# Sums of log decays: loaded broadcast for each unit, or multiplied out on TensorE (gated linear attention with a mixture of experts)

## The chip, the cores and the metric

The kernel runs on one core of a Trainium2 chip. The metric is the device time of one launch in microseconds (us); a smaller time is better. Engines are named as the profile names them: PE (TensorE), DVE (VectorE), ACT (ScalarE), POOL (GpSimd) and SP (SyncE, which here only issues DMAs). Each engine works through its own instructions in a fixed order, and stands still while the next one in that order waits.

## The reference

The input `x` has 4 sequences of 2048 tokens of 256 numbers. A layer norm gives `xn`, and the output is `x + attention(xn) + experts(xn)`. The attention is gated and linear: 8 heads, keys of 128, values of 64, and one decay per token and head.

```python
q = (x @ Wq).reshape(B, S, H, DK)
k = (x @ Wk).reshape(B, S, H, DK) * DK ** (-0.5)
v = (x @ Wv).reshape(B, S, H, DV)
alpha = jax.nn.sigmoid((x @ Wg + bg) / GATE_NORM)

def step(state, inp):
    qt, kt, vt, at = inp
    state = at[..., None, None] * state + kt[..., None] * vt[:, :, None, :]
    out_t = jnp.einsum('bhk,bhkv->bhv', qt, state)
    return (state, out_t)
...
og = jax.nn.sigmoid(x @ Wog)
return out * og @ Wo
```

The experts are 64 small gated networks (256 to 128 to 256). A router picks 8 of them for each token, an expert takes at most the first 256 tokens that picked it, and the weighted results are added to the output.

## The kernel before

**Chunked attention.** The scan is done in chunks of 128 tokens. With `L(t)` the running sum of log decays inside a chunk, the product of query `i` and key `j` of one chunk is weighted by `exp(L(i) - L(j))` where `i >= j` and by zero elsewhere. What a chunk passes on is a state of 128 by 64 for each head.

**Blocks, units, half blocks.** `block(s)` (line 1031) runs 32 times, each time over 256 tokens, which are two chunks (`ck` 0 and 1), for two halves of four heads (`half` 0 and 1). The pair (half, chunk) of a block is a *unit*: there are 128 units. A block is software pipelined in two half blocks; each ends with `outputs(done)` for two units. For one unit the work is: `unit_l` (the decay matrix `dc`, 128 keys by 4 heads by 128 queries, fp32), `unit_a` (the scores `sp` on PE), `unit_m` (line 929, DVE: `dc = sp * dc`), and in `outputs` the products of `dc` with the values and of the state with `qt` (lines 945 and 951). Around them are `keys` and `queries` (projections `pj`, each split on ACT and DVE into two fp16 parts, lines 220 and 221), `turn_keys` (transposes `kp`), `states`, `split_o` (`oh` on ACT, `ol` on POOL or DVE) and `output`.

**The decay matrix before.** `decays(gi)` makes the sums for a group of batches (`DGROUPS`; one batch is 512 tokens): it splits the log decays on a grid, sums them with PE, cuts the sums into three bf16 parts, turns them and stores them in DRAM as `lt_d`; `exp` of the sums goes to `el_d`. `load_block` (line 783) loads the parts of queries and keys into rows of `mv` and `aj`, whose other rows hold -1, 1 and 0. `unit_l` then multiplies the two, 128 by 128 by 512 in bf16 (`lp`, line 899): that gives all differences `L(i) - L(j)`. ACT applies Relu with scale -1 and then Exp with scale -1 (lines 903 and 904), and a mask clears `i < j`: POOL's `affine_select` (line 909) in the first 16 blocks, a DVE multiply by `u_le` (line 907) from then on.

**Loads broadcast over partitions.** `load_el` (line 798) loads `el`, the factors that queries are multiplied by (`qt`, line 860): one row in DRAM is copied to all 128 partitions, 512 KB for half a block. There are three buffers, so that such a load waits until an earlier `qt` has been made. `wall` (line 866) is the last column of `el`.

**Stages.** While blocks 0 to 15 run, side jobs run between their steps: `front(b)` (layer norm, split, transposes, stores), `decays` and `back(b)` (the router). After them the bank pools of PSUM are shared anew (`share_banks(3)`: three banks for `pj` in place of four), and the 64 experts run between the steps of blocks 16 to 31. Before block 0 lies a prologue in which the weights are scaled and split.

**What sets the order.** The program states work in the order of the calls; a scheduler places each instruction on its engine's queue by its own simulated times, and `tc.issue_after` ties some to others. All loads and most stores are issued on SP, in one queue. Each DMA there uses one of eight completion semaphores in turn, and waits until the DMA eight places earlier has landed.

Of the kernel before, what the change touches and what calls it, by code (L numbers as in the profile page):

```python
# [8 lines left out]
F32 = mybir.dt.float32  # L9
F32R = mybir.dt.float32r  # L10
F16 = mybir.dt.float16
BF16 = mybir.dt.bfloat16
# [30 lines left out]
CGRID = 1.5 * 2.0 ** 14  # L43
# [5 lines left out]
NPART = 3  # L49
NJ = NPART * H  # L50
KL = 2 * NJ + 2 * NPART

# [19 lines left out]
def gla_moe_kernel(ctx: ExitStack, tc: tile.TileContext, x, Wq, Wk, Wv, Wo, Wg, bg, Wog,  # L72
# [17 lines left out]
    lt_d = [dram.tile([2 * NPART, H, RT, P], BF16, name=f"lt_d{b}") for b in range(NB)]  # L90
# [4 lines left out]
    identb = const.tile([P, P], BF16, name="identb")  # L95
    nc.vector.tensor_copy(identb, ident)
# [15 lines left out]
    w_end = const.tile([P, NB, H, RT], F32, name="w_end")  # L112
# [9 lines left out]


    mz = tmpc.tile([P, H], BF16, name="mz")
    nc.vector.memset(mz, 0.0)
    for q0 in (0, NJ + 2 * NPART):
        for m in range(NPART):
            nc.gpsimd.affine_select(out=mz, in_=mz, pattern=[[-1, H]],
                                    compare_op=ALU.not_equal, fill=-1.0, base=-(q0 + 8 * m),
                                    channel_multiplier=1)  # L130
    NM = 4

    mv_t = [const.tile([P, H, P], BF16, name=f"mv{i}") for i in range(NM)]
    aj_t = [const.tile([P, NCK, P], BF16, name=f"aj{i}") for i in range(2)]
    nc.gpsimd.tensor_copy(mv_t[0], bc(mz, 2, P))
    for t in aj_t:
        nc.vector.memset(t, 1.0)
# [111 lines left out]
    dcp = ctx.enter_context(tc.tile_pool(name="dcp", bufs=2))  # L249
# [33 lines left out]

    lad = r1.tile([P, RT, P], BF16, name="lad")
# [26 lines left out]
    zs = r1.tile([P, NB, H, RT], F32, name="zs")  # L311
    sg = r1.tile([P, NB, H, RT], F32, name="sg")
# [20 lines left out]
    def front(b):  # L333
# [79 lines left out]
        nc.vector.scalar_tensor_tensor(zs[:, b].rearrange("p h t -> p t h"), in0=lg[:, :, E:E + H],  # L413
# [8 lines left out]
    def decays(gi):  # L422

        b0, nb_ = DGROUPS[gi]
        n = nb_ * H * RT

        z = zs[:, b0:b0 + nb_].rearrange("p b h t -> p (b h t)")
        sm = sg[:, b0:b0 + nb_].rearrange("p b h t -> p (b h t)")
        nc.vector.tensor_scalar(sm, sm, SMIN, None, ALU.max)
        made["ln"] = nc.scalar.activation(sm, sm, AF.Ln).ins  # L430
        nc.vector.tensor_scalar(z, z, -UMIN, 0.0, ALU.add, ALU.min)
        nc.vector.tensor_scalar(z, z, LMIN - UMIN, None, ALU.max)
        yield True
        nc.vector.tensor_tensor(z, z, sm, ALU.add)

        g = dk.tile([P, 2, n], F32, tag="g", name="g")
        nc.vector.tensor_scalar(g[:, 0, :], z, CGRID, CGRID, ALU.add, ALU.subtract)
        made["g"] = nc.vector.tensor_tensor(g[:, 1, :], z, g[:, 0, :], ALU.subtract).ins
        yield True
        cs = ps["mo"].tile([P, 4, n], F32, tag="mo", name="cs")  # L440
        nc.tensor.matmul(cs[:, 0:2, :].rearrange("p a n -> p (a n)"), lhsT=u_le,
                         rhs=g.rearrange("p a n -> p (a n)"), start=True, stop=True)
        for q in range(2):
            nc.tensor.matmul(cs[:, 3, :], lhsT=u_le, rhs=g[:, q, :], start=(q == 0), stop=(q == 1))
        made["cs"] = nc.tensor.matmul(cs[:, 2, :], lhsT=u_gt, rhs=z, start=True, stop=True).ins

        le = dk.tile([P, n], F32, tag="le", name="le")
        made["le"] = nc.scalar.activation(le.rearrange("p (b t h) -> p b h t", b=nb_, t=RT),
                                          cs[:, 3, :].rearrange("p (b h t) -> p b h t", b=nb_, t=RT), AF.Exp).ins
        made["exp"] = nc.scalar.activation(w_end[:, b0:b0 + nb_].rearrange("p b h t -> p (b h t)"),  # L450
                                           cs[:, 2, :], AF.Exp).ins
        lt = dk.tile([P, 2, nb_, NPART, H * RT], BF16, tag="lt", name="lt")
        rs = dk.tile([P, 2, n], F32, tag="g", name="rs")
        by_batch = dict(b=nb_)
        c4 = cs[:, 0:2, :].rearrange("p a (b n) -> p a b n", **by_batch)
        r4 = rs.rearrange("p a (b n) -> p a b n", **by_batch)
        nc.vector.tensor_copy(lt[:, :, :, 0, :], c4)
        nc.vector.tensor_tensor(r4, c4, lt[:, :, :, 0, :], ALU.subtract)
        nc.vector.tensor_copy(lt[:, :, :, 1, :], r4)
        nc.vector.tensor_tensor(r4, r4, lt[:, :, :, 1, :], ALU.subtract)  # L460
        made["lt2"] = nc.vector.tensor_copy(lt[:, :, :, 2, :], r4).ins
        yield True
        ep = ps["mo"].tile([n, P], F32, tag="mo", name="ep")
        nc.tensor.transpose(ep, le, ident)
        els = dk.tile([n, P], F32, tag="ls", name="els")
        nc.vector.tensor_copy(els, ep)
        nc.sync.dma_start(out=el_d[gi], in_=els)
        NR = NPART * H * RT
        for i in range(nb_):
            b = b0 + i  # L470
            lp = ps["mo"].tile([NR, 2, P], BF16, tag="mo", name="ltp")
            for q in range(2):
                made["ltp"] = nc.tensor.transpose(lp[:, q, :], lt[:, q, i].rearrange("p a n -> p (a n)"), identb).ins
            lts = r2.tile([NR, 2, P], BF16, name="lts")
            made["lts"] = nc.vector.tensor_copy(lts, lp).ins
            made["lt"] = nc.sync.dma_start(out=lt_d[b].rearrange("(q a) h c i -> (a h c) q i", q=2), in_=lts).ins
            yield True
# [305 lines left out]
    def load_block(s):  # L783
        if s:
            begin_block(s)
        b, c0 = s // 2, (s % 2) * NCK
        aj = aj_t[s % 2]
        lt = lt_d[b].rearrange("a h c i -> (a h) c i")
        nc.sync.dma_start(out=aj[0:NJ], in_=lt[0:NJ, c0:c0 + NCK, :])
        nc.sync.dma_start(out=aj[NJ + 2 * NPART:KL], in_=lt[NJ:2 * NJ, c0:c0 + NCK, :])  # L790
        mv = []
        for ck in range(NCK):
            t = mv_t[(s * NCK + ck) % NM]
            loaded = nc.sync.dma_start(out=t[NJ:NJ + 2 * NPART], in_=lt_d[b][:, :, c0 + ck, :])
            mv.append(t)
        blk[s].update(loaded=loaded, aj=aj, mv=mv)
# [32 lines left out]
    def values(s, ck):  # L829

        B = blk[s]
        b, c0 = s // 2, (s % 2) * NCK
        xh, xl = B["x"]
        vp = ps["pj"].tile([P, H, DV], F32, tag="pj", name="pj")
        for c in range(2):
            product(vp.rearrange("p h v -> p (h v)"), (xh[:, ck, c, :], xl[:, ck, c, :]),
                    (wparts["wv"][0][:, c, :], wparts["wv"][1][:, c, :]), c == 0, c == 1)
        v = vp_.tile([P, H, DV], F32, name="v")
        nc.scalar.activation(v, vp, AF.Copy, scale=VFIT)
        B["v"][ck] = v  # L840
        if (s * NCK + ck + 1) % (SEQ // P):
            vwh = vp_.tile([P, H, DV], F16, name="vwh")
            vwl = vp_.tile([P, H, DV], F16, name="vwl")
            vw = w1.tile([P, H, DV], F32, name="vw")
            B["aux"].tensor_tensor(vw, v, bc(w_end[:, b, :, c0 + ck], 2, DV), ALU.mult)
            nc.scalar.copy(vwh, vw)
            B["aux"].tensor_tensor(vwl, vw, vwh, ALU.subtract)
            B["vw"][ck] = (vwh, vwl)

# [44 lines left out]
    def unit_l(s, half, ck):  # L894

        B = blk[s]
        h0 = half * 4
        lp = ps["pj"].tile([P, 4, P], F32, tag="pj", name="lp")
        nc.tensor.matmul(lp.rearrange("p h i -> p (h i)"), lhsT=B["aj"][:, ck, :],  # L899
                         rhs=B["mv"][ck][:, h0:h0 + 4, :].rearrange("p h i -> p (h i)"),  # L900
                         start=True, stop=True)
        dc = dcp.tile([P, 4, P], F32, name="dc")
        nc.scalar.activation(dc, lp, AF.Relu, scale=-1.0)
        nc.scalar.activation(dc, dc, AF.Exp, scale=-1.0)

        if "at" in moe:
            nc.vector.tensor_tensor(dc, dc, bc(u_le, 1, 4), ALU.mult)
        else:
            nc.gpsimd.affine_select(out=dc, in_=dc, pattern=[[0, 4], [1, P]], compare_op=ALU.is_ge,
                                    fill=0.0, base=0, channel_multiplier=-1)  # L910
# [120 lines left out]
    def block(s):  # L1031
# [8 lines left out]
        if n:  # L1040
            load_block(s + 1)
            load_el(s + 1, 0)
# [31 lines left out]
        if not n:  # L1074
# [7 lines left out]
            return  # L1082
        load_el(s + 1, 1)
# [35 lines left out]
    for t in mv_t[1:]:  # L1119
        nc.sync.dma_start(out=t, in_=mv_t[0])  # L1120
# [54 lines left out]
    with after(made["el"]):  # L1175
        load_block(0)
    with after(blk[0]["loaded"].ins):
        load_el(0, 1)
        nc.sync.dma_start(out=gbias, in_=gate_bias.partition_broadcast(P))
# [13 lines left out]
    with after(blk[0]["loaded"].ins):  # L1193
# [72 lines left out]
```

## Time and profile before

| | |
|---|---|
| median of 3 runs | 1252.58 us (1251.79 to 1253.54) |
| profiled execution: time | 1252.01 us |
| profiled execution: span on the core | 1250.0 us |
| granted clock of PE, mean | 0.995 |
| busy: PE, DVE, ACT, POOL | 1191.4, 973.5, 857.5, 709.3 us |
| moved by DMA | 165.35 MB |

The profile is of one execution. Its span of 1250.0 us is the part in which the core's engines run; 2.0 us lie around it. Busy time of PE counts each matmul from its start to its modelled end, and matmuls overlap, so that a duration is longer than the step from one start to the next. A line of a group reads: line of the kernel, engine, operation, output<-inputs, shape and type, count, then busy time, mean duration in ns, and the idle time of the engine just before these instructions with what ended it.

### The profile page before, as it was taken

Reading aid. Unit: us, or ns where it says so; the run is one execution under the profiler, and the core shown is the slowest. Engines: PE = TensorE matmul, PEld = TensorE weight load, DVE = VectorE, ACT = ScalarE, POOL = GpSimd, SP = SyncE. Lnnn points to the kernel's source line nnn. Section 1 sums busy time; section 2 is a strip of 40 time slices with the busy share of each in tenths; the row PEclk is TensorE's granted clock in tenths of the full one; section 3 lists DMA queues with packets and bytes.
Section 4 is the critical chain, followed back from the end, with each engine's and each line's share of the span. In section 5 each row is a group of like instructions: output and inputs, shape, how many; then the busy total and the mean of one; then the engine's idle time right before and its main releaser. Section 6 shows DMA issues by size and latency. Waiting matters only on the chain.

```text
span 1250.0 us, 34808 instructions
## 1 busy us (share of the span) xinstructions
PE 1191.4 (95%) x13783; PEld 1040.7 (83%) x13783; DVE 973.5 (78%) x2669; ACT 857.5 (69%) x1536; POOL 709.3 (57%) x899
## 2 busy tenths in 40 slices
PE   6799999989999999999899999999999999999997
PEld 6587888877888878878789989999988898998986
DVE  6987778786787877777878878787878788887674
ACT  4567666666667567654667777777777777778764
POOL 1476667765666566653426656637757567565330
PEclk9899999999999999999999999999999999999999
DMA  7434444434334443323637676767767678666531
GB/s 244 158 123 127 131 122 117 126 87 114 97 112 127 135 127 110 108 52 78 181 87 152 163 160 137 169 151 178 157 156 167 148 167 180 150 138 150 111 60 35
DMA packets 148579, 165.35 MB, mean 132 GB/s; under 512 B 32384, under 2 KB 119296, under 8 KB 147712
## 3 DMA queue, kind: packets, MB, share of 16 engines
q1 hardware_dynamic: 114896, 113.57, 29.6%
q0 software_dynamic: 29712, 45.89, 21.5%
q10 hardware_dynamic: 3808, 3.67, 0.8%
q8 instruction: 108, 1.77, 0.6%
q14 instruction: 55, 0.45, 0.1%
HBM read 115.98 MB, written 58.38 MB: 139 GB/s over the span
## 4 chain that ended last, share of the span: by engine, by line
PE 68%; DVE 13%; POOL 6%; ACT 5%; DMA 5%; issue 3%; SPq 1%; DVEq 0%; POOLq 0%; ACTq 0%
PE pj L269 11%; PE pj L271 11%; PE pj L270 11%; PE od L945 4%; PE kp L884 3%; PE od L951 3%; DMA el<-el_d 3%; PE gu L269 2%; PE gu L271 2%; PE gu L270 2%; PE xet L646 2%; PE sp L270 2%; PE sp L269 2%; PE sp L271 2%; PE lp L899 1%
## 5 line engine op out<-in xcount | busy, mean ns | idle before, releaser
L702 POOL DMA_INDIRECT out_dram<-y,idx x128 | 211.6, 1653 | 93.1 <-issue 25.4
L626 POOL DMA_INDIRECT xe<-xw_d,idx x128 | 133.5, 1043 | 127.2 <-ACT y L688 86.9
L269 PE MATMUL pj<-xs,wq_h 128*128 128x256 f16 x496 | 135.4, 273 | 6.6 <-DVE k L221 4.6
L269 PE MATMUL pj<-xs,wk_h 128*128 128x256 f16 x496 | 135.6, 273 | 0.0
L271 PE MATMUL pj<-xs,wk_l 128*128 128x256 f16 x496 | 135.5, 273 | 0.0
L270 PE MATMUL pj<-xs,wk_h 128*128 128x256 f16 x496 | 135.5, 273 | 0.0
L270 PE MATMUL pj<-xs,wq_h 128*128 128x256 f16 x496 | 135.2, 273 | 0.0
L271 PE MATMUL pj<-xs,wq_l 128*128 128x256 f16 x496 | 135.2, 273 | 0.0
L929 DVE TENSOR_TENSOR dc<-sp,dc 128x512 f32<-128x512 f32 x128 | 87.7, 685 | 45.8 <-PE sp L271 28.4
L221 DVE SCALAR_TENSOR_TENSOR k<-pj,k 128x512 f16<-128x512 f32 x128 | 87.1, 683 | 40.1 <-ACT k L220 40.1
L220 ACT ACTIVATE k<-pj 128x512 f16<-128x512 f32 x128 | 75.2, 591 | 55.4 <-PE pj L271 55.1
L945 PE MATMUL od<-dc,v 128*64 128x128 f32 x1024 | 101.5, 280 | 7.3 <-DVE dc L929 7.3
L270 PE MATMUL sp<-ql,k 128*128 128x128 f16 x512 | 96.1, 220 | 5.5 <-DVE ql L221 5.2
L269 PE MATMUL sp<-qh,k 128*128 128x128 f16 x512 | 98.2, 220 | 0.0
L271 PE MATMUL sp<-qh,k 128*128 128x128 f16 x512 | 96.1, 220 | 0.0
L220 ACT ACTIVATE qh<-pj 128x512 f16<-128x512 f32 x128 | 76.0, 597 | 27.0 <-PE pj L271 26.8
L951 PE MATMUL od<-qt,state 128*64 128x128 f32 x960 | 94.4, 273 | 0.0
L989 ACT CAST oh<-oT 128x512 fp32r<-128x512 f32 x64 | 39.6, 618 | 79.5 <-DVE oT L959 79.5
L221 DVE SCALAR_TENSOR_TENSOR ql<-pj,qh 128x512 f16<-128x512 f32 x128 | 86.8, 679 | 9.2 <-ACT qh L220 9.1
L716 DVE TENSOR_TENSOR wl<-w,wh 128x768 fp32r<-128x768 f32 x64 | 61.2, 956 | 40.9 <-ACT wh L650 39.3
L884 PE MATMUL kp<-identh,k 128*128 128x128 f16 x1024 | 83.0, 220 | 8.7 <-DVE k L221 5.4
L860 DVE SCALAR_TENSOR_TENSOR qt<-pj,el 128x512 f32<-128x512 f32 x128 | 86.7, 678 | 0.0
(408 smaller groups left out, 4533.6 us busy)
## 6 DMA issues: line engine op xcount, KB each, us to landing
el<-el_d SPq DMA_DIRECT2D x64, 512.0 KB
xw_d<-x SPq DMA_DIRECT2D x16, 512.0 KB
xT_d<-xT SPq DMA_DIRECT2D x16, 512.0 KB
out_dram<-in_L_attn_x_dram SPq DMA_DIRECT2D x16, 512.0 KB
w<-in_L_ffn_w_gate_dram SPq DMA_DIRECT2D x64, 128.0 KB
w<-in_L_ffn_w_up_dram SPq DMA_DIRECT2D x64, 128.0 KB
w<-in_L_ffn_w_down_dram SPq DMA_DIRECT2D x64, 128.0 KB
xs<-xT_d SPq DMA_DIRECT2D x31, 256.0 KB
```

The lines of the kernel that those rows point to most:

```text
L220: return (nc.scalar.activation(hi, t, AF.Copy, scale=scale).ins, nc.vector.scalar_tensor_tensor(lo, in0=t, scalar=scale, in1=hi, op0=ALU.m ...
L221: nc.vector.scalar_tensor_tensor(lo, in0=t, scalar=scale, in1=hi, op0=ALU.mult, op1=ALU.subtract).ins)
L269: nc.tensor.matmul(out_, lhsT=a[0], rhs=b[0], start=first, stop=False)
L270: nc.tensor.matmul(out_, lhsT=a[0], rhs=b[1], start=False, stop=False)
L271: return nc.tensor.matmul(out_, lhsT=a[1], rhs=b[0], start=False, stop=last).ins
L626: in_turn(lambda: nc.gpsimd.indirect_dma_start(out=xe[:, f, :], out_offset=None, in_=xw_d[:, :], in_offset=bass.IndirectOffsetOnAxis(ap=id ...
L702: two = [in_turn(lambda: nc.gpsimd.indirect_dma_start(out=of, out_offset=bass.IndirectOffsetOnAxis(ap=idx[:, e, f:f + 1], axis=0), in_=m[" ...
L860: read = nc.vector.scalar_tensor_tensor(qt, in0=pj, scalar=QFIT, in1=two_heads(el, i), op0=ALU.mult, op1=ALU.mult)
L884: nc.tensor.transpose(kp[:, i, :], k[:, i, :], identh)
L929: anchor.append(nc.vector.tensor_tensor(dc, B["sp"], dc, ALU.mult).ins)
L945: mm = nc.tensor.matmul(od[i * DV:(i + 1) * DV, n, j, :], lhsT=v[:, h0 + 2 * j + i, :], rhs=dc[:, 2 * j + i, :], start=True, stop=first)
L951: mm = nc.tensor.matmul(od[i * DV:(i + 1) * DV, n, j, :], lhsT=state[half][:, 2 * j + i, :], rhs=qt[:, ck, 2 * j + i, :], start=False, sto ...
```

## The change

`decays` no longer splits the sums. With the log decays `z` (tokens by batch, chunk and head) it makes three sums with PE in fp32: after the token (`w_end` as before), up to the token (`el` as before), and `nl`, which is minus the sum from the start of the token's own group of 32 keys (`GQ` = 4 groups of `Q` = 32). One more product, `z` against a constant `tq`, gives for each of the four groups the sum from the group's start to the query, and it is stored in DRAM as `la_d`. `load_la` copies the rows of one unit to the partitions: four DMAs of 64 KB, each of 2 KB to 32 partitions. `unit_l` masks the loaded tile first (to -3e4; POOL as before, or a DVE minimum), and then takes four Exps of 128 columns, one for each head, with `nl` as bias. The matmul `lp`, the Relu, the tiles `mv` and `aj` and their loads are gone. The tile `la` takes the place of `dc` and has six buffers in place of two. In `block`, `load_la` is called for the units two half blocks ahead.

```diff
-        g = dk.tile([P, 2, n], F32, tag="g", name="g")
-        nc.vector.tensor_scalar(g[:, 0, :], z, CGRID, CGRID, ALU.add, ALU.subtract)
-        made["g"] = nc.vector.tensor_tensor(g[:, 1, :], z, g[:, 0, :], ALU.subtract).ins
...
+        cs = ps["mo"].tile([P, 3, n], F32, tag="mo", name="cs")
+        for k, u in enumerate((u_gt, u_le, uq)):
+            made["cs"] = nc.tensor.matmul(cs[:, k, :], lhsT=u, rhs=z, start=True, stop=True).ins
...
+        made["lt2"] = nc.vector.tensor_copy(nl[:, b0:b0 + nb_].rearrange("p b t h -> p (b t h)"), cs[:, 2]).ins
...
+        lp = ps["mo"].tile([n, GQ, P], F32, tag="mo", name="lap")
+        made["ltp"] = nc.tensor.matmul(lp.rearrange("n g i -> n (g i)"), lhsT=z,
+                                       rhs=tq.rearrange("p g i -> p (g i)"), start=True, stop=True).ins
+        las = dk.tile([n, GQ, P], F32, tag="las", name="las")
+        made["lts"] = nc.vector.tensor_copy(las, lp).ins
+        made["lt"] = nc.sync.dma_start(out=la_d[gi].rearrange("g n i -> n g i"), in_=las).ins
...
-        for ck in range(NCK):
-            t = mv_t[(s * NCK + ck) % NM]
-            loaded = nc.sync.dma_start(out=t[NJ:NJ + 2 * NPART], in_=lt_d[b][:, :, c0 + ck, :])
...
+    def load_la(s, half, ck):
+
+        b, c = s // 2, (s % 2) * NCK + ck
+        la = lap.tile([P, 4, P], F32, name="la")
+        gi = max(i for i, g in enumerate(DGROUPS) if g[0] <= b)
+        r = ((b - DGROUPS[gi][0]) * RT + c) * H + half * 4
+        src = la_d[gi][:, r:r + 4, :].rearrange("g h i -> g (h i)")
+        for g in range(GQ):
+            made["la"] = nc.sync.dma_start(out=la[g * Q:(g + 1) * Q].rearrange("p h i -> p (h i)"),
+                                                 in_=src[g].partition_broadcast(Q)).ins
+        sums[s, half, ck] = la
...
     def unit_l(s, half, ck):
...
-        nc.tensor.matmul(lp.rearrange("p h i -> p (h i)"), lhsT=B["aj"][:, ck, :],
-                         rhs=B["mv"][ck][:, h0:h0 + 4, :].rearrange("p h i -> p (h i)"),
-                         start=True, stop=True)
-        dc = dcp.tile([P, 4, P], F32, name="dc")
-        nc.scalar.activation(dc, lp, AF.Relu, scale=-1.0)
-        nc.scalar.activation(dc, dc, AF.Exp, scale=-1.0)
-
+        b, c = s // 2, (s % 2) * NCK + ck
+        dc = sums.pop((s, half, ck))
         if "at" in moe:
-            nc.vector.tensor_tensor(dc, dc, bc(u_le, 1, 4), ALU.mult)
+            nc.vector.tensor_tensor(dc, dc, bc(later_, 1, 4), ALU.min)
         else:
             nc.gpsimd.affine_select(out=dc, in_=dc, pattern=[[0, 4], [1, P]], compare_op=ALU.is_ge,
-                                    fill=0.0, base=0, channel_multiplier=-1)
+                                    fill=NONE, base=0, channel_multiplier=-1)
+        for i in range(4):
+            hh = half * 4 + i
+            nc.scalar.activation(dc[:, i], dc[:, i], AF.Exp, bias=nl[:, b, c, hh:hh + 1])
...
         if n:
-            load_block(s + 1)
+            begin_block(s + 1)
...
+            load_la(s + 1, 0, 1)
+            load_la(s + 1, 1, 0)
             load_el(s + 1, 0)
...
+        load_la(s + 1, 1, 1)
+        if 0 < s < NS - 2:
+            load_la(s + 2, 0, 0)
         load_el(s + 1, 1)
...
-    for t in mv_t[1:]:
-        nc.sync.dma_start(out=t, in_=mv_t[0])
```

In the changed program's queues, each new tile's loads on SP wait for the `outputs` products that last read its buffer, those of the half block just ended. Its mask stands a few instructions behind the following `ol` (on DVE in the stage of the experts, on POOL before it), and its four Exps stand on ACT between the splits of keys and queries of that same half block, two half blocks before `unit_m` uses them.

## The prediction, made before the changed kernel ran

> **What bounds the kernel now.** I read the busy times first, then the stages, then the chain of waits.
>
> ```profile
> PE 1191.4 (95%) x13783; PEld 1040.7 (83%) x13783; DVE 973.5 (78%) x2669; ACT 857.5 (69%) x1536; POOL 709.3 (57%) x899
> core 0: us, PE busy (x) PEld busy (x) DVE busy (x) ACT busy (x) POOL busy (x), PEclk, DMA share, GB/s
> 50.10:604.60 554.50, 522.86 (x6284) 441.99 (x6285) 435.72 (x1278) 359.90 (x646) 344.65 (x602) 0.99 0.40 115
> 604.60:1208.80 604.20, 601.91 (x6835) 541.29 (x6833) 477.50 (x1219) 452.11 (x815) 351.96 (x262) 1.00 0.66 149
> PE 68%; DVE 13%; POOL 6%; ACT 5%; DMA 5%; issue 3%; SPq 1%; DVEq 0%; POOLq 0%; ACTq 0%
> ```
>
> PE carries the chain: 68% of the span, and in the stage of the experts (604.6 to 1208.8) it is never without a matmul. Before that stage (50.1 to 604.6) PE is covered to 94% only, and DVE, POOL, ACT and DMAs stand on the chain between its pieces. In both stages DVE and ACT have a fifth or more of their time free.
>
> Next the rows that the change touches, from the groups, and how matmuls follow each other, from the timeline of PE.
>
> ```profile
> L904 ACT ACTIVATE dc<-dc 128x512 f32<-128x512 f32 x128 | 81.2, 634 | 2.2
> L903 ACT ACTIVATE dc<-lp 128x512 f32<-128x512 f32 x128 | 76.1, 595 | 14.3 <-PE lp L899 14.3
> L899 PE MATMUL lp<-mv,aj 128*128 128x512 bf16 x128 | 49.3, 386 | 0.0
> L907 DVE TENSOR_TENSOR dc<-dc,u_le 128x512 f32<-128x512 f32 x63 | 43.2, 686 | 4.3 <-ACT dc L904 3.7
> 831.94 0.38 PE L899 MATMUL lp<-mv,aj 128*128 128x512 bf16 x1
> 832.15 0.27 PE L269 MATMUL pj<-xs,wk_h 128*128 128x256 f16 x1
> ```
>
> `lp` is listed with 386 ns, but the next matmul starts 0.21 us after it. So 49.3 us is not what its removal can give: 128 x 0.215 us = 27.5 us is.
>
> **The change, part by part.**
>
> *PE.* 128 `lp` go: 65 up to the expert stage (14.0 us of steps), 60 in it (12.9), 3 at the end. The pieces of the chain, summed by stage, hold 5.9 us of `lp` before the expert stage, 11.6 in it and 1.1 after it. I take the chain's numbers; the ends are 27.5 us (all of it) and 0 (something else is late at once). The sums in `decays` change by a few matmuls for six groups: nothing. `pj` has one tile less to pass through its banks for each unit. In the half block after 831 us the second product of queries starts at 839.67, 0.12 us after DVE released a `pj` bank (838.86 + 0.69): with three banks such a wait is near, and without `lp` the bank is one product older (some 1.4 us). That is slack for what follows, not time by itself.
>
> *ACT.* Relu and Exp of 512 columns follow each other by 0.48 and 0.53 us: 1.01 us a unit. Four Exps of 128 columns take their place, each with a bias read from SBUF. The nearest row has the shape, a read pointer (as scale) and SBUF as source:
>
> ```profile
> 13.01 0.39 ACT L220 ACTIVATE gwz<-gate_f,fit 128x128 f16<-128x128 f32 x1
> 13.30 0.29 ACT L220 ACTIVATE gwz<-wg_f,fit 128x16 f16<-128x16 f32 x1
> ```
>
> The next starts 0.29 us later: 4 x 0.29 = 1.16 us, 0.15 more a unit, 19 us in all. The ends are 4 x 0.10 (64 columns without a pointer, 129.22 to 129.32) and 4 x 0.49 (256 columns with two pointers, line 386), that is -78 and +122 us of ACT. ACT has 1250.0 - 857.5 = 392 us free, so 0 on the path; without that cover 19 us.
>
> *Masks.* The DVE minimum costs what the multiply did (686 ns), POOL's select what it did (636 ns): 0. But they now stand ahead of the Exps, and wait for a DMA.
>
> *DVE in `decays`.* Five cuts and two grid steps a group and sixteen copies of about 0.28 us go, six larger copies come: some 11 us less, off the path, 0.
>
> *DMA.* 128 tiles of 256 KB are 33.5 MB, less 1.6 MB of parts: 32 MB more. The queue moved 113.57 MB in 29.6% of the engines' span, so 8.3% more; the share in the expert stage goes from 0.66 to about 0.75. No engine is full: 0 by itself.
>
> *SP.* 512 issues of about 0.42 us (as `w` loads follow each other) replace 128 of 0.35 to 0.76: 215 against 71 us, and SP does nothing else. Moved past on its queue are `el`, `xs` and the experts' `w` loads. The first are needed a half block later; `w` is loaded two casts ahead (lines 633 and 650), against 3.4 us for eight issues. 0.
>
> *The new wait.* SP issues the loads of two tiles when the `outputs` products of the half block are done. The tile's mask follows `ol` on DVE (POOL before the experts), behind it stand the `k` split and the experts' `hl` and `hs`; on ACT the Exps stand ahead of `k` and `qh`, for which PE waits. In the half block after 831.0 us that place is 2.7 us after the last product that reads `dc`:
>
> ```profile
> 833.41 0.42 DVE L981 TENSOR_TENSOR state<-state,wall 128x256 f32<-128x256 f32 x1
> 833.94 0.69 DVE L907 TENSOR_TENSOR dc<-dc,u_le 128x512 f32<-128x512 f32 x1
> ```
>
> The tile is there after 4 x 0.42 = 1.7 us of issue plus the landing of the last piece. No row shows such a load. The low end is the 48 KB store of `lt_d` (1.52 us in the chain), the high end `el`, 512 KB, also a broadcast:
>
> ```profile
> 135.90 0.36 SPq L804 DMA_DIRECT2D el<-el_d  x1
> 141.88 0.19 POOL L866 COPY wall<-el 128x8 f32<-128x8 f32 x1 [1.92 <-DMA el<-el_d]
> 185.18 0.39 SPq L804 DMA_DIRECT2D el<-el_d  x1
> 188.96 0.27 POOL L866 COPY wall<-el 128x8 f32<-128x8 f32 x1 [0.68 <-DMA el<-el_d]
> ```
>
> That is 3.8 us alone and 6.0 behind other bulk. A 64 KB piece is nearest to the store in size: I take 2.0 us, so the first tile lands at 3.7 us, 1.0 us late, and the second at 5.4, about in time. The bank slack above (about 1.4 us) takes up 1.0 us. I count 4 us for half blocks in which bulk stores are ahead; the ends are 0 and what the first rival gives.
>
> The Trainium skill, page "DMA: Bandwidth & Descriptors", "Rules for kernel authors", speaks against the four pieces: it says that transfers to disjoint parts of the partitions are not worth it, and that one transfer to 128 partitions should be used. Its "Anatomy of one DMA" gives a fixed cost of about 2.0 us for each DMA on the GpSimd path. If four pieces paid that in turn, a tile would take an estimated 8 us, and the first rival would hold; the `w` loads above are issued 0.42 us apart without waiting for each other.
>
> *Prologue.* The first `od` starts at 50.05, after POOL's mask had waited for `el` (issued at 43.05, behind eleven other issues from 36.69 on). In the changed order the first mask needs only the first `la`, issued right after the first `el`: it could be done near 40, and the first products some 6 us earlier. But 24 more issues (10 us of SP) now stand ahead of the `el` of block 1, and POOL waits for it in order. I take -3, ends -6 and +4.
>
> **Sum.** -3 (prologue) - 5.9 - 11.6 - 1.1 (`lp`) + 4 (late tiles) = -17.6. Span 1250.0 becomes 1232.4, the profiled time 1252.01 becomes 1234.4; the median of the runs stood 0.6 above it: 1235.
>
> **Rivals.**
>
> *First, slower: the tile lands late and blocks two engines in order.* Place: the mask on DVE or POOL and the Exps on ACT, ahead of the splits for which PE waits. For it: all 22 waits of POOL for `el` (33.8 us) are of this kind, a reader placed where the scheduler thought the data would be. Against: the pieces are an eighth of `el`. It decides where a piece takes over 2.4 us to land: then the tile is over 1.4 us late and the rest goes to PE in all 63 half blocks. At 3.3 us that is 0.9 x 63 = 57 us, less the 21.6 us of gains: +35, 1288. At 2.7 us it is 19 us and no change.
>
> *Second, the time goes to others.* Before the expert stage PE has gaps already; if DVE and ACT set that stage, its 5.9 us and the prologue's 3 give nothing, and ACT's 19 us are partly seen: 11.6 less about 10, 1251.
>
> *Third, more is released.* All 27.5 us of steps plus 6 in the prologue: 1219. For it: `lp` held a bank, and ACT waited 14.3 us for it. Against: the gaps before the expert stage.
>
> *That the loads are not ahead at all* is the first rival with a higher price.
>
> **How the numbers follow.** The forecast (own range 1224 to 1247) has 0.43, the first rival above 1255 has 0.36, the second (1247 to 1256) 0.12, the third 0.09. What a measurement of this kernel can tell from no change is about 0.2%, 2.5 us: faster is below 1250.1. Faster: 0.43 + 0.09 + 0.04 = 0.56; same 0.07; slower 0.37. The range from 1221 to 1285 leaves out about 0.1 on each side.
>
> **What would show it.** Right: no `lp`, PE's step sum about 27 us less, `la` Exps near 0.39 us, 0.29 apart, DVE and POOL waiting for `la` DMAs under 1 us a tile, PE still covered in the expert stage, first `od` before 50. Wrong: waits of DVE line 872 or POOL line 874 for `la` of 2 us or more, ACT idle ahead of its Exps, and gaps of PE that end with `k`, `ql` or `hs`. Then the first rival holds. If PE has gaps without such waits, the second does.

## The result, and the profile after

The changed kernel takes 1301.08 us (median of 4 runs, 1298.49 to 1303.39) against 1253.06 us of the kernel before on the same chip: ratio 1.0377, 95% interval 1.0347 to 1.0408. It is 48 us slower where 18 us faster was forecast. The profiled execution took 1303.39 us, with a span of 1301.3. All medians, ranges and ratios here are of fast runs: one run of the experiments (1268.65 us, masks tied on DVE and POOL) was over 1.5% above the fastest of its kernel and is not counted.

First the page of the changed kernel: busy times, chain, and the groups of the new Exps and the new mask.

```profile
PE 1196.6 (92%) x13623; PEld 1036.9 (80%) x13623; DVE 970.5 (75%) x2625; ACT 864.7 (66%) x1792; POOL 712.4 (55%) x892
...
PE 41%; DMA 18%; DVE 15%; ACT 10%; SPq 6%; issue 4%; POOL 2%; DVEq 0%; POOLq 0%; ACTq 0%
...
L878 ACT ACTIVATE la<-la,nl 128x128 f32<-128x128 f32 x512 | 163.7, 391 | 124.8 <-DVE la L872 71.0
...
L872 DVE TENSOR_TENSOR la<-la,later 128x512 f32<-128x512 f32 x63 | 44.0, 698 | 78.6 <-DMA la<-la_d 72.0
```

Then its two stages, before the experts and with them (length, busy time of PE, PEld, DVE, ACT and POOL, granted clock, DMA share, GB/s).

```profile
47.40:579.30 531.90, 490.68 (x5831) 412.40 (x5829) 413.52 (x1187) 348.94 (x748) 335.54 (x592) 0.98 0.51 144
579.30:1241.40 662.10, 622.67 (x6937) 552.89 (x6936) 491.86 (x1263) 464.61 (x951) 354.37 (x268) 0.98 0.70 163
```

No engine became the bound: DVE, ACT and POOL are about as long busy as before. PE fell from 68% to 41% of the chain, DMAs rose from 5% to 18%. In the stage of the experts PE had been covered for 601.91 of 604.20 us; now it is covered for 622.67 of 662.10. (The two stretches don't hold quite the same work, 6835 and 6937 matmuls, so what was lost is read from the table further down.) The last column of the groups, the idle time ahead of the instruction, names who: DVE's mask idles for the load, ACT's Exp idles for DVE's mask.

The changed kernel's view of waits (engine, line, releaser: total us, times, longest us):

```profile
DVE la L872 <- DMA la<-la_d: 72.0, 40, 6.2
ACT la L878 <- DVE la L872: 71.0, 45, 6.4
POOL wall L837 <- DMA el<-el_d: 57.9, 26, 4.7
ACT la L878 <- POOL la L874: 53.3, 37, 4.2
...
POOL la L874 <- DMA la<-la_d: 37.6, 30, 3.3
...
PE pj L255 <- DVE k L207: 12.0, 7, 4.6
```

DVE and POOL together wait 109.6 us for `la`, and ACT waits behind both. One half block of the expert stage, one of its worst, shows how this reaches PE (timelines of the queues and engines; start, duration, and in brackets the idle time and its releaser):

```profile
849.30 0.95 POOL L984 DMA_DIRECT2D out_dram<-at_d  x1 [10.03 <-DMA at_d<-res]
...
850.81 3.81 SPq L765 DMA_DIRECT2D la<-la_d  x8
...
855.09 0.28 DVE L577 TENSOR_SCALAR before<-srow,cex 128x256 f16<-128x256 f16 x1
...
859.29 0.69 DVE L872 TENSOR_TENSOR la<-la,later 128x512 f32<-128x512 f32 x1 [3.92 <-DMA la<-la_d]
...
859.90 0.68 DVE L207 SCALAR_TENSOR_TENSOR k<-pj,k 128x512 f16<-128x512 f32 x1
...
860.02 1.28 ACT L878 ACTIVATE la<-la,nl 128x128 f32<-128x128 f32 x4 [2.96 <-DVE la L872]
...
860.64 0.28 PE L255 MATMUL pj<-xs,wq_h 128*128 128x256 f16 x1 [0.65 <-DVE k L207]
```

SP issues both tiles from 850.81 on, just behind a 1 MB store. DVE is done at 855.4 and stands at the mask until 859.29. Behind it in order is the `k` split (859.90), which frees a `pj` bank, and PE waits for that bank. The tile itself is needed only two half blocks later (line 897 multiplies it at 906.5): of the six tiles, four are masked already and wait for their use, and two are being loaded; the scheduler, which goes by its own times, put the mask of the newest pair right here.

Over the 32 half blocks of the expert stage, the first mask waited for its load in 29. In these it started 4.9 us (median; 3.6 to 9.8) behind the first issue of its load, and 2.9 us (median) behind the end of its fourth, worked out from the timelines of SP and DVE.

Where the time was lost, as the start of `oT` (line 927) in a half block, less the same start before (us; half block 0 is the first with an output, 30 is near the end of the stage before the experts). The other two columns are experiments told below, made where the kernel before took the same (1254.49 us).

| half block | before, at | after | masks tied on DVE | no loads |
|---|---|---|---|---|
| 0 | 51.74 | -4.35 | -4.97 | +0.50 |
| 10 | 224.76 | +14.40 | +9.15 | +2.18 |
| 30 | 569.72 | +9.56 | +3.93 | -3.40 |
| 46 | 894.72 | +26.86 | -3.26 | -13.07 |
| 62 | 1223.89 | +54.46 | -7.94 | -20.03 |

The prologue gained, ten half blocks lost 19 us, and the expert stage lost 45 more. That loss is uneven: six of its 32 half blocks lost 3.3 to 8.5 us each, 31 us together, and the other 26 lost 14. In three of the six (4.2, 8.5 and 3.8 us) a 1 MB store (line 984) was issued just ahead of the loads, as in the half block shown, and their first masks stood 8.5 to 11.1 us behind the first issue, the three longest times of all (the profile puts the longest down to a load of `w`).

The waits come with a second loss, on PE. After the mask of 859.29, PE waits for `k` once more, and then the granted clock is at a half: matmuls of `gu` that started 0.11 us apart start 0.21 us apart. First PE's timeline, then two such stretches (last columns: granted clock, DMA share, GB/s):

```profile
864.18 0.61 PE L855 MATMUL kp<-identh,k 128*128 128x128 f16 x8 [1.94 <-DVE k L207]
...
865.25 0.28 PE L255 MATMUL gu<-xe,wh 128*128 128x256 f32 x1
865.36 0.28 PE L256 MATMUL gu<-xe,wh 128*128 128x256 f32 x1
...
866.26 0.41 PE L255 MATMUL gu<-xe,wh 128*128 128x256 f32 x1
866.47 0.41 PE L256 MATMUL gu<-xe,wh 128*128 128x256 f32 x1
```

```profile
865.60:869.00 3.40, 3.40 (x21) 3.21 (x20) 3.27 (x9) 1.85 (x5) 2.79 (x3) 0.51 0.71 124
1046.50:1053.30 6.80, 4.25 (x25) 4.16 (x26) 6.29 (x19) 3.86 (x9) 5.52 (x5) 0.50 0.71 148
```

Between half blocks 30 and 62 the changed kernel has six such stretches, 27.3 us in all, and five of them lie in the six half blocks that lost most. The kernel before, the one with masks tied on DVE and the one without loads have none there. PE was busy for 22.5 us of the six; at half the rate that is some 11 us of work lost, an estimate from these rows. What sets a stretch off was not tested.

### The profile page after: what moved, and what is told of

Same layout as the page of the kernel before. It is cut to its first block, busy times and chain, and to the rows that moved or that the text cites. A ratio compares the mean times of both kernels' runs of the same rounds, so it can differ in the third digit from the quotient of the medians.

```text
span 1301.3 us, 35781 instructions
## 1 busy us (share of the span) xinstructions
PE 1196.6 (92%) x13623; PEld 1036.9 (80%) x13623; DVE 970.5 (75%) x2625; ACT 864.7 (66%) x1792; POOL 712.4 (55%) x892
## 2 busy tenths in 40 slices
DMA packets 165786, 196.89 MB, mean 151 GB/s; under 512 B 33072, under 2 KB 120496, under 8 KB 164912
## 4 chain that ended last, share of the span: by engine, by line
PE 41%; DMA 18%; DVE 15%; ACT 10%; SPq 6%; issue 4%; POOL 2%; DVEq 0%; POOLq 0%; ACTq 0%
DMA la<-la_d 12%; PE pj L255 7%; PE pj L257 6%; PE pj L256 6%; SPq L765 6%; ACT la L878 4%; PE od L913 3%; PE kp L855 2%; DMA xs<-xT_d 2%; PE od L919 2%; DVE ql L207 2%; DVE qt L831 2%; PE gu L256 2%; PE gu L255 2%; PE gu L257 2%
## 5 line engine op out<-in xcount | busy, mean ns | idle before, releaser
L878 ACT ACTIVATE la<-la,nl 128x128 f32<-128x128 f32 x512 | 163.7, 391 | 124.8 <-DVE la L872 71.0
L255 PE MATMUL pj<-xs,wq_h 128*128 128x256 f16 x496 | 137.6, 277 | 12.8 <-DVE k L207 12.0
L256 PE MATMUL pj<-xs,wq_h 128*128 128x256 f16 x496 | 137.3, 277 | 0.0
L255 PE MATMUL sp<-qh,k 128*128 128x128 f16 x512 | 100.8, 222 | 11.1 <-ACT qh L206 8.9
L913 PE MATMUL od<-la,v 128*64 128x128 f32 x1024 | 101.4, 280 | 6.3 <-DVE la L897 5.8
L897 DVE TENSOR_TENSOR la<-sp,la 128x512 f32<-128x512 f32 x128 | 87.3, 683 | 21.5 <-PE sp L257 21.2
L872 DVE TENSOR_TENSOR la<-la,later 128x512 f32<-128x512 f32 x63 | 44.0, 698 | 78.6 <-DMA la<-la_d 72.0
L855 PE MATMUL kp<-identh,k 128*128 128x128 f16 x1024 | 87.4, 222 | 15.8 <-DVE k L207 12.0
L257 PE MATMUL sp<-qh,k 128*128 128x128 f16 x512 | 97.4, 221 | 0.0
L855 PEld LDWEIGHTS <-k 128*128 128x128 f16 x1024 | 67.8, 99 | 25.6 <-issue 12.0
```

The costliest lines, as they stand in the source:

```text
L255: nc.tensor.matmul(out_, lhsT=a[0], rhs=b[0], start=first, stop=False)
L256: nc.tensor.matmul(out_, lhsT=a[0], rhs=b[1], start=False, stop=False)
L257: return nc.tensor.matmul(out_, lhsT=a[1], rhs=b[0], start=False, stop=last).ins
L855: nc.tensor.transpose(kp[:, i, :], k[:, i, :], identh)
L878: nc.scalar.activation(dc[:, i], dc[:, i], AF.Exp, bias=nl[:, b, c, hh:hh + 1])
L897: anchor.append(nc.vector.tensor_tensor(dc, B["sp"], dc, ALU.mult).ins)
```

## Experiments

Three theories: **A**, the first rival of the prediction, a tile lands late and blocks DVE, POOL and ACT in order; **B**, the 32 MB and 384 issues more hold up the other transfers; **C**, the four Exps are too long for ACT. Runs were made in four groups; each group is compared with the kernel before on its own chip. That kernel took 1254.49 us in the first group, 1296.26 and 1296.89 in the second and third, which ran on one chip, and 1283.34 in the fourth. So times are compared within a group only.

**First group: what is the wait made of.**

*Masks tied later (pin).* In `unit_l`, around the mask:

```
+        with ExitStack() as late:
+            if anchor:
+                late.enter_context(tc.issue_after(anchor[-1]))
```

> Loads, bytes, issues and the four Exps stay as in the changed kernel; only the mask of each tile is tied behind the last product of scores with decays that is already stated (line 897), so that mask and Exps stand about 17 us behind the issue of their loads instead of 4 to 5 us. Theory A (a tile lands late and blocks DVE, POOL and ACT in order): the 109.8 us that DVE and POOL wait for these loads fall under 15, and the time falls from 1301 to 1230 to 1250. Theory B (the 32 MB and 384 issues more hold up the other transfers): nothing of that changes, 1290 or more. Theory C (four Exps a tile are too much for ACT): 1290 or more.

Measured: 1240.88 us (1240.59 to 1243.26), ratio 0.9896 (0.9871 to 0.9921): 60 us less than the changed kernel, by nothing but the place of 63 masks and of their Exps. The mask now stands some 12 us ahead of its tile's use, a median of 38 us behind the first issue (not 17, as was expected). No wait of DVE's mask for `la` is left. Of this run the chain on its page, POOL's wait, and the expert stage:

```profile
PE 60%; DMA 10%; DVE 10%; ACT 7%; POOL 3%; SPq 3%; issue 3%; POOLq 0%; ACTq 0%; DVEq 0%
```

```profile
POOL la L877 <- DMA la<-la_d: 36.5, 29, 3.2
```

```profile
604.40:1225.00 620.60, 618.39 (x7093) 557.84 (x7094) 492.15 (x1256) 468.80 (x965) 357.71 (x262) 1.00 0.72 171
```

PE is covered again (618.39 of 620.60), with the same bytes at a DMA share of 0.72. B and C fall as main cause. POOL's 36.5 us stayed, so that the waits did not all fall as expected: the tie is to an instruction on DVE and orders that engine's queue alone, and POOL's masks stand as early as before.

*No loads (noload).* `for g in range(GQ)` in `load_la` becomes a range of 0 for all tiles but the first, and the mask reads `bc(u_le, 1, 4)`.

> All loads of the tiles but the first are left out, and the mask reads a constant in their place, so the decays are wrong; masks and four Exps a tile stay, with nothing to wait for. Theories A and B: both lose their cause, 1220 to 1245. Theory C: 1285 or more. With the run in which the masks are tied later, the difference between these two is what traffic and issues cost (A: under 10 us; B: 40 or more).

Measured: 1229.31 us (1227.50 to 1231.23), ratio 0.9801 (0.9774 to 0.9827). That is what the change is worth without its loads: 25 us less than before. C falls for good: all 512 Exps are there. It is also 11.6 us less than with tied masks, where under 10 was expected; POOL's early masks and the loads themselves are in this difference.

*One Exp (exp1).* The loop of four Exps becomes `nc.scalar.activation(dc, dc, AF.Exp)`.

> One Exp of 512 columns without bias takes the place of the four; the sum of the key is left out of the decays. Loads and masks stay where they are. Theory A: the wait for the load stays, ACT's part behind it is shorter by 4 x 0.32 - 0.53 = 0.7 us a unit: 1275 to 1300. Theory C: the four Exps cost the 54 us and more, 1235 to 1255.

Measured: 1291.93 us (1289.15 to 1293.88), ratio 1.029 (1.0262 to 1.0317). DVE still waits 80.8 us for `la` (72.0 in the changed kernel). Shorter Exps give 9 us; they stand behind the late mask and ahead of `k`, so a part of their length is on the path there. They are not the main cause.

*One DMA for a tile (one).*

```
-        for g in range(GQ):
-            made["la"] = nc.sync.dma_start(out=la[g * Q:(g + 1) * Q].rearrange("p h i -> p (h i)"),
-                                                 in_=src[g].partition_broadcast(Q)).ins
+        made["la"] = nc.sync.dma_start(out=la.rearrange("p h i -> p (h i)"), in_=bc(src, 1, Q)).ins
```

> Each tile is loaded by one DMA to all 128 partitions instead of four pieces of 32; 128 issues instead of 512, the bytes and the place of the masks unchanged. Theory A: the first tile's mask started 5.0 us (median of the expert stage) behind the first issue, of which three issues of 0.42 us are 1.3 us. If a whole tile lands as fast as a piece, 1.3 us of some 1.9 us of waiting per half block goes: 1240 to 1265. If it lands as slowly as the 512 KB el (3.8 us alone, 6.0 behind others), little goes: 1285 to 1305. Theory B: issues on SP matter: 1270 or less; if bytes alone matter, 1300. Theory C: 1300.

Measured: 1514.90 us (1510.02 to 1516.25), ratio 1.2065 (1.2028 to 1.2101): far outside of all that was expected. The waits for `la` grew to 310.6 us. The packets on the pages tell why; first the changed kernel, then this run:

```profile
DMA packets 165786, 196.89 MB, mean 151 GB/s; under 512 B 33072, under 2 KB 120496, under 8 KB 164912
```

```profile
DMA packets 158101, 196.82 MB, mean 130 GB/s; under 512 B 25392, under 2 KB 112816, under 8 KB 157232
```

And a stretch of this run's prologue in which these loads stand alone (last columns: granted clock, share of the 16 DMA engines, GB/s):

```profile
45.00:46.00 1.00, 0.10 (x1) 0.00 (x0) 0.00 (x0) 0.00 (x0) 0.00 (x0) 0.84 0.25 96
46.00:47.00 1.00, 0.00 (x0) 0.00 (x0) 0.00 (x0) 0.00 (x0) 0.07 (x1) 1.00 0.27 102
```

A quarter of the engines' time is used, at some 100 GB/s, with nothing else under way. Small packets fell by (33072 - 25392) / 128 = 60 a tile, which fits 4 x 16 before and 4 now, one for each engine of each DMA. The DMA reads four rows, each broadcast to 32 partitions, and ran as on four engines. The run without loads, which keeps one tile's, agrees: (33072 - 24944) / 127 = 64 small packets a tile with four pieces. The Trainium skill, page "DMA: Bandwidth & Descriptors", "Rules for kernel authors", says this in its rule on using all 16 engines: an outermost dimension smaller than 16 confines the whole DMA to at most that many. Row and rule agree.

**Second group: POOL's masks, and one row for all partitions.**

*Masks tied on DVE and POOL (pin2).* As pin, and also behind `splits[-1:]`, which holds the last `vwl` (line 818, on POOL before the experts).

> Up to the expert stage the masks stand on POOL, where the tie to a DVE product did nothing (POOL waited 36.5 us for these loads, as in the changed kernel), and between the first and the eleventh half block both kernels lost some 14 us that the kernel without loads did not. Here POOL's masks are tied behind the split of the weighted values (line 818) of the half block before, and DVE's masks as in the run before. Theory A (the place of the masks): POOL's waits fall under 8 us, and the loss up to the eleventh half block shrinks to 2 to 5 us: 1226 to 1235. Theory B (32 MB and 384 issues more slow the other transfers, of el above all, while DMAs are busy early): the loss stays, 1238 to 1244.

*One reference row (g1).* `GQ = 4` becomes `GQ = 1`: one DMA from one row loads a tile.

> One group of 128 rows instead of four of 32 (one reference row for the sums of a half block, so a tile is one row for all partitions and one DMA loads it); masks stand early, as in the changed kernel. In the run with one DMA from four rows a tile took 132 packets, which is 128 and 4, where four pieces took 192, which is four times 32 and 16. If the last numbers are the DMA engines that shared the work, one row for all partitions takes 128 and 16, and the tile lands in 3 to 4 us from its issue instead of 8: 1245 to 1275, below the changed kernel. If a single DMA of 256 KB is slow as such: near 1515.

*Both (pin2g1).*

> Both: masks tied later on DVE and POOL, and one DMA for a tile. Theory A: once the mask stands 15 us behind the issue, the landing does not matter, and 384 issues fewer on SP gain little: within 4 us of the run with the ties alone. Theory B: issues on SP cost, 5 to 12 us less than with the ties alone.

*One Exp under tied masks (pin2exp1).* pin2 with the edit of exp1.

> Ties as in the first of these, and one Exp of 512 columns without bias for the four, so that the key's sum is left out of the decays. If ACT's longer work is off the path, as the forecast has it: within 3 us of the run with the ties alone. If a part of it is on the path: 5 to 20 us less.

Measured: pin2 1251.81 us (1246.72 to 1260.05), ratio 0.9665 (0.9613 to 0.9717); g1 1325.89 (1322.21 to 1330.51), 1.0244 (1.0186 to 1.0302); pin2g1 1256.78 (1250.28 to 1260.97), 0.9696 (0.9652 to 0.9740); pin2exp1 1247.36 (1242.55 to 1251.92), 0.9638 (0.9582 to 0.9693). The limits in us, set on the first chip, did not fit this one; by the ratios the ties gained more than expected, and g1 missed: it is no better than the changed kernel was on the same chip (1.0228, third group). The last two do not differ measurably from pin2: 384 issues fewer on SP bring nothing that shows, and ACT's longer work is covered where its mask is not late (4 us by the medians, with intervals that overlap). The packets of g1, and the same stretch of its prologue:

```profile
DMA packets 158101, 196.04 MB, mean 148 GB/s; under 512 B 26928, under 2 KB 112816, under 8 KB 157232
```

```profile
45.00:46.00 1.00, 0.00 (x0) 0.00 (x0) 0.15 (x1) 1.00 (x5) 0.82 (x2) 1.00 1.07 392
46.00:47.00 1.00, 0.00 (x0) 0.00 (x0) 1.00 (x9) 1.00 (x5) 0.21 (x1) 1.00 1.06 391
```

Here (33072 - 26928) / 128 = 48 small packets a tile are gone, which leaves 16, and the engines are full at 390 GB/s (loads of `el`, each from one row too, and of the weights of `wo` share this stretch with the tiles). Yet the instructions on these tiles still idle for their loads for 102.8 us in all (310.6 with four rows).

**Third group: the same four side by side.**

> The changed kernel itself, beside the next three: 1.034 to 1.041 of the kernel before.

> DVE's masks tied later, POOL's not: 0.987 to 0.992 of the kernel before, as in its first run.

> DVE's and POOL's masks tied later, now beside the run with DVE's alone. Theory A (place of the mask): 5 to 9 us less than that, since POOL's waits for the loads fell from 36.5 to 2.0 us. Theory B (bytes and issues): the same within 2 us.

> One row for all partitions, one DMA a tile, masks early. In the prologue of the run with four rows in one DMA, loads alone kept the DMA share at 0.25 to 0.27 and some 100 GB/s; with one row 1.04 to 1.10 and 390 GB/s. If issue and landing of the first tile are what the early mask waits for, its first mask comes 4.5 us behind the first issue instead of 4.9: 5 to 25 us below the changed kernel. If not, the same as the changed kernel.

| kernel | us (range) | ratio to before (95%) |
|---|---|---|
| changed kernel (after_b) | 1328.71 (1320.98 to 1331.97) | 1.0228 (1.0185 to 1.0271) |
| masks tied on DVE (pin_b) | 1266.16 (1262.39 to 1268.33) | 0.9749 (0.9721 to 0.9777) |
| tied on DVE and POOL (pin2_b) | 1255.36 (1248.53 to 1259.48) | 0.9661 (0.9629 to 0.9693) |
| one reference row, masks early (g1_b) | 1318.66 (1306.04 to 1323.33) | 1.0172 (1.0137 to 1.0206) |

On this chip the change costs 2.3%, and the two ties are worth 63 and 11 us. The changed kernel and the tie on DVE alone fell below the ratios that were expected from the first chip; the second tie gave a little more than its 5 to 9 us. The waits for `la` under both ties, against 55.4 us of DVE's mask and 41.9 of POOL's in the changed kernel beside it, and then the chain on the page of the run with both ties:

```profile
DVE la L901 <- DMA la<-la_d: 5.9, 3, 3.0
...
POOL la L878 <- DMA la<-la_d: 2.0, 1, 2.0
```

```profile
PE 72%; DVE 8%; ACT 6%; DMA 6%; POOL 3%; issue 3%; SPq 1%; another core or an unknown queue 0%; DVEq 0%; ACTq 0%; POOLq 0%
```

Loading from one row instead of four helps little by comparison: the first mask stands 4.4 us behind the first issue (5.4 with four pieces), DVE's mask still waits 69.9 us, and the two intervals overlap. A mask placed right behind its load waited for it in each of the three ways of loading that were tried.

**Fourth group: what the loads themselves cost.** The place was settled, the loads' own price not.

> Masks tied late on DVE and POOL, as before, here for comparison with the next two: 0.962 to 0.985 of the kernel before.

> No loads but the first, masks read a constant (the decays are wrong), as before. If the place of the mask was the whole loss, it is within 4 us of the kernel with tied masks. If traffic and issues cost as well, it is 8 us or more below it.

The third takes the kernel without loads, with `w_end` as the bias of the Exps, and adds, in `load_la`:

```
+            made["la"] = nc.sync.dma_start(out=unread[ck][g * Q:(g + 1) * Q],
+                                                 in_=src[g][0:488].partition_broadcast(Q)).ins
+            if "od" in made:
+                tc.add_manual_dep(made["la"], made["od"].name, ...)
```

> As without loads (masks read a constant, and the bias of the Exps another sum, so the decays are wrong), but all 512 loads are issued behind the products of the half block, into two tiles that nobody reads (488 of 512 columns each, 5% fewer bytes). If traffic and issues are free, as the forecast has it: within 4 us of the kernel without loads. If they delay the transfers of el, xs and the experts' weights: 8 to 20 us above it.

Measured: no loads 1242.68 us (1241.35 to 1247.36), ratio 0.9704 (0.9673 to 0.9735); loads that nobody reads 1250.52 (1245.39 to 1251.97), 0.9749 (0.9715 to 0.9782); tied masks 1253.29 (1246.28 to 1257.39), 0.9772 (0.9736 to 0.9808). The kernel without loads is 10.6 us below the one with tied masks. By the medians the loads cost about 8 us by themselves, between the two limits that were set for it and with intervals that overlap a little; so they are probably not free, but this does not settle it. The far larger part of the loss was the place of the masks (60 us by the tie on DVE in the first group, 73 by both in the third). Of the 8 us, 4.2 stand already at half block 8, where this run's loads came earlier in the prologue; how much of it is the steady traffic stays open.

## Why the prediction was wrong

**The step that failed is the new wait, counted at 4 us.** It put the first tile at 3.7 us behind its first issue, 1.0 us late, and let 1.4 us of slack absorb that. Both halves failed. The first tile's mask could start 4.9 us (median) behind the first issue: the last piece took 2.9 us to land, not 2.0, and the four issues some 2.0, not 1.7. The 2.0 was chosen because a 64 KB piece is nearest in size to the 48 KB store of `lt_d`, at 1.52 us in the prologue; but the chain of the kernel before holds another of these stores:

```profile
414.68 3.90 DMA lt_d<-lts
```

`el`, which is loaded the same way, broadcast and behind bulk, was at 3.8 and 6.0 from its issue on. Either row would have put the tile past the slack.

**The slack was also read too well.** Its 1.4 us came from one half block. In the expert stage DVE waited 72.0 us for its tiles, and from half block 30 to 62 the changed kernel lost 61.5 us against the kernel without loads (54.46 - 9.56 here, -20.03 + 3.40 there). Some 11 us of that are the slow clock and at most 8 the loads themselves, both estimates from above. So 42 to 61 of the 72 us reached PE directly, and the slack took up 0.3 to 0.9 us a half block. A wait of 3.92 us, as in the half block shown, can't be taken up by it, and the longest was 6.2.

**The first rival** had named the place, the mechanism and the point from which it decides (2.4 us); the mechanism is shown by the tied masks. Its size came near in part by luck. It priced 3.3 us of landing at 1288; at the 2.9 measured, its own sum gives 0.5 x 63 - 21.6 = +10 us, while the kernel came to 1301, 48 us above. It too subtracted the slack, spread the loss evenly over both stages, and had no term for the slow clock.

**Part by part.** Removing `lp`: forecast 18.6 us in the three stages and 3 in the prologue; without loads 25 us were gained (3.9 before the experts, 16.6 with them, 3.4 in the tail by the table's starts and the spans), which lies between the 18.6 of the chain's pieces and the 27.5 of all steps. Exps: 391 ns and 0.30 apart, as forecast (0.29), and not measurably on the path while the mask is not late; 9 us were where it was. Masks: 698 ns on DVE and 637 on POOL, as forecast. SP's issue: median 419 ns, as forecast (0.42), and 384 issues fewer gained nothing that shows. DMA: 31.5 MB more, as forecast, at a share of 0.70 in the expert stage (0.75 forecast); taken as 0, it was some 8 us or less. Prologue: forecast -3, measured -4.35; but from half block 0 to 10 the kernel then lost 19 us, which no term held. Without loads it lost 2 there. POOL's wait for `el`, named with an end of +4, rose from 33.8 to 57.9 us in all, but it is not shown to be the cause: with one Exp a tile it was 20.0 us, and 13 us were lost over the same half blocks.

**The Trainium skill's rule on disjoint partition halves** (same page and section), weighed in the prediction against the four pieces, was not what decided: one transfer from four rows took 1515 us instead of 1301; one transfer from one row 10 us less than four pieces, which the intervals do not separate. That four pieces would pay a fixed cost in turn (an estimated 8 us a tile) did not show: first issue to mask was 4.9 us. What spoke against this change was where the load was waited for, not that it came in four pieces.

## What to carry to other kernels

When a load takes the place of a product, ask first where its reader stands in the in-order queue: a reader that a scheduler puts right behind its load holds up all that follows it on its engine, however far ahead of its use the data is loaded. Loading two half blocks ahead hid nothing until the reader was tied near its place of use; then the same loads made the kernel 1.0% faster than before instead of 3.8% slower on the first chip, and 3.4% faster with POOL's masks tied as well on the second. Size a landing by rows of the same kind at the same place (a broadcast behind bulk stores), not by one from the prologue, and set the worst half blocks, not the median, against the slack: here six half blocks held 31 of 45 us.

## What was not expected of the hardware

One DMA whose source has four rows ran on a quarter of the DMA engines (share 0.25 to 0.27, some 100 GB/s) where loads from one row for all partitions, those of `el` among them, filled them (1.04 to 1.10, some 390 GB/s), at the same 256 KB a tile to 128 partitions. The waits also came with stretches in which PE ran at half its clock (0.50 and 0.51, matmuls 0.21 us apart instead of 0.11), an estimated 11 us beside the waits themselves. And the same kernel before took 1254 us on one chip and 1283 to 1297 in the other groups; in the third the change cost 2.3% instead of 3.8%. Why stays open.
